# Gated feed-forward of a small transformer layer: the last 42 columns of gate and value as one block of weights

## The chip, the cores and the metric

The kernel runs on one core of one Trainium2 chip. The core has five engines that work side by side and wait for each other through semaphores: TensorE (PE in the profile; its weight loads are listed as PEld), VectorE (DVE), ScalarE (ACT), GpSimd (POOL) and SyncE (SP, which here only issues loads and stores). Matrix products land in PSUM, from where VectorE and ScalarE read them; everything else lies in SBUF. Each engine runs its instructions strictly in the order of the program. The metric is the device time of one execution in microseconds; the median of several runs is compared.

## The reference, cut to what matters

The whole computation is two layers of a model on 32 sequences of 64 positions and 256 channels, with a context of 1601 rows for each sequence. Layer 1 has a cross-attention over the context, then a block with a causal convolution, a gated recurrence and a gated feed-forward, then a quantised feed-forward. The change concerns the gated feed-forward alone:

```
FF_INNER = int(D * 4 * 2 / 3)          # D = 256, so 682
...
n = _rmsnorm(x, ff_gamma)
ff = jax.nn.silu(n @ w_gate) * (n @ w_value) @ w_ff_out
x = ff * RES_SCALE + x
```

`w_gate` and `w_value` are 256 x 682, `w_ff_out` is 682 x 256. The 682 inner channels are five blocks of 128 and a rest of 42.

## The kernel before, in words

The 2048 rows of x are cut into 16 tiles of 128 rows (two sequences each). They are processed in the order 1, 2, ..., 15, 0; this text calls them by these numbers. The long loop of the program runs over pieces of the context: 13 for each tile, each with a fixed order on TensorE: the scores with the maxima taken off (`s`, lines 770 and 776), the values of a later piece (`vps`), the scores by rows of a piece five ahead (`r`, line 728), whose maxima VectorE takes (line 735, `mx`), the weighted sums of values (`o`, line 800), and the keys of a piece six ahead (`kps`). `s` and `r` take turns in two buffers of PSUM of their own.

All other work of the two layers is written as generators that `yield` between their steps. A list named `plan` gives each generator a start, an end and a count of steps, and the loop runs the steps that are due at two places of each piece: between `vps` and `r`, and after `kps`. The order of instructions on TensorE, VectorE, ScalarE and GpSimd is the order in which this Python code runs; the scheduler moves nothing on these four. Only the order on SyncE is its own.

The work on several tiles is under way at once: while the gated block of tile t is computed, the first layer of tiles t+3 and t+4 and the query of tile t+3 are too, so that between `vps` and `r` there may stand, one behind the other, the feed-forward of one tile, the transposition `tp_d` (for the query) of another, and a step of a third.

The small products all take their PSUM tiles from one pool, `ps_mm`, of three buffers (`mm_tile`). A tile's buffer is given on when the last instruction that reads it has run. Which buffer the next tile is laid into, and so which reader its first matmul waits for, is settled when the program is built, by the building framework. In the program before, the second half's two tiles and the two that follow lie, for tile 1, in buffers 0, 1, 2 and 0: `ff_1_3_0` in 0, `ff_1_3_1` in 1, `tp_d` in 2, and `tp_c` again in 0, where it waits for the reading of line 235.

The gated feed-forward (generator `recurrent`, from line 938) works on `nT`, the normalised tile transposed: 128 channels x 2 chunks x 128 rows. The inner channels are padded from 682 to 6 x 128 (`NF` is 6); the padding of `w_fg` (gate) and `w_fv` (value) is zeroed once by GpSimd (line 1046), and the rest is loaded by SyncE (line 1056) in the function `late_weights`, in the first 40 us. The six blocks are done in two halves of three. For each half, one PSUM tile holds three blocks of gate sums and another three blocks of value sums (`ff_<tile>_<first block>_0` and `_1`). Each block is two matmuls (one for each chunk of channels, `mm2`), and each fp32 matmul is two records in the trace: 24 records a half. Then `silu_mul` (lines 234 to 238): ScalarE takes tanh of half the gate; VectorE halves the gate (line 235), multiplies it by the value (line 236), and after a `yield` by tanh + 1 (line 238). Since both read the same PSUM tile, VectorE's line 235 waits for ScalarE's line 234. At last `ffo` (line 951) multiplies the six blocks `m` by `w_fo`, whose rows beyond 682 are zero.

Of the kernel before, what the change touches and what calls it, by code (L numbers as in the profile page):

```python
# [9 lines left out]
F32 = mybir.dt.float32  # L10
BF16 = mybir.dt.bfloat16
AF = mybir.ActivationFunctionType
ALU = mybir.AluOpType
AX = mybir.AxisListType

P = 128
# [8 lines left out]
FF = 682  # L25
NF = 6
# [18 lines left out]
def perceiver_kernel(ctx: ExitStack, tc: tile.TileContext, a: dict, out: bass.AP):  # L45
    nc = tc.nc
    PSUM = bass.MemoryType.PSUM

    const = ctx.enter_context(tc.tile_pool(name="const", bufs=1))
# [20 lines left out]
    def mm_tile(shape, name, dtype=F32):  # L70
        return ps_mm.tile(shape, dtype, tag="mm", name=name)
# [111 lines left out]
    def moments(x, name):  # L183

        st = small.tile([P, 6], F32, tag="bnst", name=f"st_{name}")
        nc.vector.bn_stats(st, x)
        mv = small.tile([P, 2], F32, tag="bnmv", name=f"mv_{name}", bufs=4)
        nc.vector.bn_aggr(mv, st)
        rstd = small.tile([P, 1], F32, tag="rstd", name=f"rstd_{name}", bufs=4)
        nc.gpsimd.tensor_scalar(rstd, mv[:, 1:2], 1e-5, None, ALU.add)  # L190
        nc.gpsimd.tensor_tensor(rstd, rstd, mhalf, ALU.pow)
        return x, mv, rstd
# [34 lines left out]
    def mm2(o, lhsT, rhs):  # L227

        for c in range(2):
            nc.tensor.matmul(o, lhsT=lhsT(c), rhs=rhs(c), start=(c == 0), stop=(c == 1))  # L230

    def silu_mul(m, u, v, th):

        nc.scalar.activation(th, u, AF.Tanh, scale=0.5)
        nc.vector.tensor_scalar(m, u, 0.5, None, ALU.mult)
        nc.vector.tensor_tensor(m, m, v, ALU.mult)
        yield
        nc.vector.scalar_tensor_tensor(m, th, 1.0, m, ALU.add, ALU.mult)
# [611 lines left out]
    def recurrent(ti, x):  # L850
        def tile_(shape, tag, name):
            return work_tile(shape, tag, f"{name}_{ti}")

        m = moments(x, f"e{ti}")
# [8 lines left out]
        for c in range(2):  # L863
            nc.scalar.activation(ypad[:, c, :, 3:], t[:, c, :].rearrange("p (b s) -> p b s", b=2), AF.Copy,
                                 scale=gains[:, c, 0:1])
# [17 lines left out]
        nT = tile_([P, 2, P], "xTb", "nT")  # L883
# [14 lines left out]
        for part in range(2):  # L898
            for c in range(2):
                for h in range(2):  # L900
                    r = slice(64 * h, 64 * h + 64)
# [34 lines left out]
        nT = tile_([P, 2, P], "xTb", "nT2")  # L936
# [1 line left out]
            nc.scalar.activation(nT[:, c, :], t[:, c, :], AF.Copy, scale=gains[:, c, 2:3])  # L938
        yield ACT
        m = tile_([P, NF, P], "w4k", "fm")  # L940
        for f0 in range(0, NF, 3):
            uv = [mm_tile([P, 3, P], f"ff_{ti}_{f0}_{j}") for j in range(2)]
            for o, w in zip(uv, (w_fg, w_fv)):
                for f in range(3):
                    mm2(o[:, f, :], lambda c: w[:, c, (f0 + f) * P:(f0 + f + 1) * P], lambda c: nT[:, c, :])
            th = tile_([P, 3, P], "g2k", f"fth{f0}")
            yield from silu_mul(m[:, f0:f0 + 3, :], uv[0], uv[1], th)
            yield ACT if f0 == 0 else None
        o = mm_tile([P, D], f"ffo_{ti}")
        for f in range(NF):  # L950
# [54 lines left out]
    def tail(ti, x):  # L1005
        x = yield from recurrent(ti, x)
        yield from bit_ffn(ti, x)
# [32 lines left out]
    w_hg = const.tile([P, 2, 2 * DI], F32, name="w_hg")  # L1040
    w_go = const.tile([P, 4, 64], F32, name="w_go")
    nc.gpsimd.memset(w_go[DI:], 0.0)
    w_fg = const.tile([P, 2, NF * P], F32, name="w_fg")
    w_fv = const.tile([P, 2, NF * P], F32, name="w_fv")
    for w in (w_fg, w_fv):
        nc.gpsimd.memset(w[:, :, FF:], 0.0)
    w_fo = const.tile([P, NF, D], F32, name="w_fo")
    nc.gpsimd.memset(w_fo[:, NF - 1, :], 0.0)

    def late_weights():  # L1050
        nc.sync.dma_start(w_o2, a["L1_xattn_WoT"].rearrange("(c p) o -> p c o", p=P))
        nc.sync.dma_start(w_pw, a["L1_attn_pw_wT"].rearrange("(c p) o -> p c o", p=P))
        nc.sync.dma_start(w_hg, a["L1_attn_w_hg"].rearrange("(c h) d e -> (h d) c e", c=2))
        nc.sync.dma_start(w_go[:DI], a["L1_attn_w_out"].rearrange("h e o -> e h o"))
        for w, name in ((w_fg, "L1_attn_w_gate"), (w_fv, "L1_attn_w_value")):
            nc.sync.dma_start(w[:, :, :FF], a[name].rearrange("(c p) f -> p c f", p=P))
        last = (NF - 1) * P
        nc.sync.dma_start(w_fo[:, 0:NF - 1, :], a["L1_attn_w_ff_out"][0:last, :].rearrange("(f p) o -> p f o", p=P))
        nc.sync.dma_start(w_fo[0:FF - last, NF - 1, :], a["L1_attn_w_ff_out"][last:FF, :])

# [159 lines left out]
    with tc.manual_schedule(engines={ET.PE, ET.DVE, ET.Activation, ET.Pool}):  # L1220
# [43 lines left out]
        for g in range(NU * NT):  # L1264
            pos, p = divmod(g, NU)
# [79 lines left out]
```

## Time and profile before

| what | value |
|---|---|
| median of 3 runs | 2155.64 us (2155.49 to 2157.81) |
| the profiled execution's own time | 2154.58 us |
| its span, first to last instruction | 2152.9 us |
| TensorE busy / weight loads | 2034.8 us / 1482.9 us |
| VectorE, ScalarE, GpSimd busy | 1302.2, 907.1, 324.7 us |
| matmul records of ff (w_fg + w_fv) | 384 + 384 |
| L234 tanh, L235, L236, L238 on 128x384 | 490, 557, 553, 547 ns (median), 32 each |
| L236 on 128x256 (the first layer's `m`) | 421 ns |
| idle time of DVE before L235, ended by L234 | 44.4 us in 32 times |

A line of the timeline has the start and the duration in us, the engine, the line of the kernel, the operation, what it writes and what it reads, the shapes and the count of merged instructions; in brackets stands how long the engine had been idle before and who ended that. Matmuls overlap one another: the duration of one record is longer than its distance to the next. A row of a table by windows has the window, its length, the busy time of PE, PEld, DVE, ACT and POOL with their counts, the granted clock of TensorE (1.00 is full speed), the DMA engines' share and GB/s.

### The profile page before, as it was taken

The page shows a single profiled execution, that of the slowest core. Times are in us where ns is not written, and L with a number is a line of the kernel's source. Part 1 is how long each engine was busy: PE and PEld are TensorE (multiplying, and loading weights), DVE is VectorE, ACT ScalarE, POOL GpSimd, SP SyncE. Part 2 cuts the span into 40 slices and gives each one's busy share as a digit, 9 for nine tenths or more (in the row PEclk, how much of TensorE's full clock was granted, in tenths as well). Part 3 has the DMA queues.
Part 4 walks back from the last instruction along what each step waited for, and adds up shares of the span by engine and source line. Part 5 has one row for each costly group of instructions (what it writes and reads, how often), then busy time and mean ns, then how long its engine had stood idle before and what let it go on. Part 6 is the DMA issues. An engine that isn't in the chain of part 4 may idle for free.

```text
span 2152.9 us, 69473 instructions
## 1 busy us (share of the span) xinstructions
PE 2034.8 (95%) x31691; PEld 1482.9 (69%) x31707; DVE 1302.2 (60%) x2614; ACT 907.1 (42%) x1400; POOL 324.7 (15%) x538
## 2 busy tenths in 40 slices
PE   5799999999999999999999999999999999999964
PEld 4567677777776777777777777767776666676753
DVE  4556756666656665665666656565676656565544
ACT  3334454444535444444444435453433334334332
POOL 2211211111112111112111111111100111000011
PEclk8799999999999999999999999999999999999986
DMA  7233212221212222112221212211111111101000
GB/s 267 84 107 115 95 66 75 68 75 35 74 67 71 73 68 67 45 66 75 68 75 40 91 33 79 75 38 42 45 45 32 47 42 35 54 2 45 2 14 5
DMA packets 52654, 134.77 MB, mean 63 GB/s; under 512 B 12894, under 2 KB 32776, under 8 KB 52360
## 3 DMA queue, kind: packets, MB, share of 16 engines
q1 hardware_dynamic: 51800, 129.52, 17.6%
q8 instruction: 248, 4.06, 0.8%
q10 hardware_dynamic: 560, 0.81, 0.1%
q14 instruction: 46, 0.38, 0.1%
HBM read 124.02 MB, written 6.29 MB: 61 GB/s over the span
## 4 chain that ended last, share of the span: by engine, by line
PE 84%; DVE 9%; ACT 3%; DMA 2%; issue 1%; POOL 1%; SPq 0%; POOLq 0%; DVEq 0%; ACTq 0%
PE vps L230 17%; PE kps L230 16%; PE r L728 10%; PE o L800 9%; PE s L776 8%; PE ff L230 4%; DVE mx L735 3%; PE s L770 3%; PE ffo L951 2%; PE q L230 1%; ACT pt L782 1%; PE wo L230 1%; PE hg L902 1%; PE s L330 1%; PE v L316 1%
## 5 line engine op out<-in xcount | busy, mean ns | idle before, releaser
L735 DVE TENSOR_REDUCE mx<-r 128x2 f32<-128x1024 f32 x384 | 451.9, 1219 | 131.2 <-PE r L728 131.1
L782 ACT ACTIVATE pt<-s 128x1024 f32<-128x1024 f32 (+1 forms) x416 | 403.0, 1020 | 286.0 <-PE s L776 285.8
L695 ACT ACTIVATE kt<-kps,chv 128x512 f32<-128x512 f32 x192 | 131.9, 687 | 636.1 <-PE kps L230 636.1
L230 PE MATMUL kps<-ctxT,w_L_xattn_WkT 128*128 128x512 f32 x768 | 384.5, 624 | 11.9 <-DMA ctxT<-ctxT 11.9
L230 PE MATMUL vps<-w_L_xattn_WvT,ctxT 128*128 128x128 f32 x3072 | 394.5, 282 | 0.0
L230 PEld LDWEIGHTS vps<-w_L_xattn_WvT,ctxT 128*128 128x128 f32 x3072 | 358.5, 192 | 23.7 <-issue 2.8
L712 DVE COPY vau<-vps 128x512 f32<-128x512 f32 (+1 forms) x208 | 143.4, 689 | 370.4 <-PE vps L230 370.4
L800 PEld LDWEIGHTS o<-pt,vau 128*32 128x32 f32 (+1 forms) x13312 | 196.7, 110 | 151.5 <-issue 139.7
L800 PE MATMUL o<-pt,vau 128*32 128x64 f32 (+1 forms) x13312 | 231.2, 221 | 5.3 <-ACT pt L782 5.2
L728 PE MATMUL r<-kt,qbd 32*128 32x512 f32 x1536 | 230.3, 650 | 1.9 <-DVE mx L735 1.1
L230 PEld LDWEIGHTS kps<-ctxT,w_L_xattn_WkT 128*128 128x128 f32 x768 | 132.0, 191 | 124.4 <-issue 107.5
L776 PEld LDWEIGHTS s<-qbd,kt 32*128 32x128 f32 x6144 | 206.2, 187 | 3.1
L776 PE MATMUL s<-qbd,kt 32*128 32x128 f32 x6144 | 207.3, 271 | 0.0
L242 ACT ACTIVATE part<-part 128x1601 f32<-128x1601 f32 x60 | 92.6, 1543 | 16.9 <-DMA part<-ctxT 16.6
L728 PEld LDWEIGHTS r<-kt,qbd 32*128 32x128 f32 x1536 | 65.7, 185 | 40.8 <-issue 18.5
L770 PE MATMUL s<-neg,onesb 3*128 3x512 bf16 x768 | 80.4, 385 | 6.7 <-DVE mx L735 4.5
L770 PEld LDWEIGHTS <-onesb 3*128 3x128 bf16 x768 | 20.9, 91 | 94.2 <-issue 92.5
L230 PE MATMUL ff<-nT,w_fg 128*128 128x128 f32 x384 | 51.7, 287 | 1.0 <-ACT nT L938 1.0
L308 POOL TENSOR_TENSOR kbd<-kT,mask 128x512 f32<-128x512 f32 x32 | 32.7, 1043 | 129.9 <-ACT kT L301 129.9
L230 PEld LDWEIGHTS ff<-nT,w_fg 128*128 128x128 f32 x384 | 47.8, 200 | 1.9 <-ACT nT L938 1.8
L230 PE MATMUL ff<-nT,w_fv 128*128 128x128 f32 x384 | 48.9, 278 | 0.0
L230 PEld LDWEIGHTS ff<-nT,w_fv 128*128 128x128 f32 x384 | 46.5, 196 | 0.0
(329 smaller groups left out, 2435.7 us busy)
## 6 DMA issues: line engine op xcount, KB each, us to landing
ctxT<-ctxT SPq DMA_DIRECT2D x32, 1601.0 KB
part<-ctxT SPq DMA_DIRECT2D x60, 800.5 KB
od<-osb SPq DMA_DIRECT2D x16, 256.0 KB
rest<-ctxT SPq DMA_DIRECT2D x32, 65.0 KB
x<-x SPq DMA_DIRECT2D x16, 128.0 KB
rs<-od SPq DMA_DIRECT2D x32, 64.0 KB
og<-od SPq DMA_DIRECT2D x32, 64.0 KB
out<-x SPq DMA_DIRECT2D x16, 128.0 KB
```

The lines of the kernel that those rows point to most:

```text
L230: nc.tensor.matmul(o, lhsT=lhsT(c), rhs=rhs(c), start=(c == 0), stop=(c == 1))
L242: nc.scalar.activation(junk, src, AF.Copy, accum_out=csum[:, c, b:b + 1])
L308: nc.gpsimd.tensor_tensor(kbd[oc], kT[:, oc, :].rearrange("p (b k) -> p b k", b=2).unsqueeze(2).to_broadcast([P, 2, 4, S]), mask4.unsqueez ...
L695: nc.scalar.activation(kt, o, AF.Identity, bias=chv[:, hf.oc, BK2:BK2 + 1])
L712: nc.vector.tensor_copy(v[:kr, :, 0:VW - 16].rearrange("p k (h d) -> p k h d", d=17)[:, :, :, 0:16], o[:kr].rearrange("p k (h d) -> p k h ...
L728: nc.tensor.matmul(o, lhsT=qbd[r, q % 2, q // 2].rearrange("p h q -> p (h q)"), rhs=w.kt[r, q, :] if h is None else halves[h].kt[k][r, :], ...
L735: nc.vector.tensor_reduce(w.mx[:, 2 * m:2 * m + 2, h % 4, k], ps[m], AX.X, ALU.max)
L770: nc.tensor.matmul(o, lhsT=onesb[r, :], rhs=halves[h].neg[r, :].unsqueeze(1).to_broadcast([3, 4, P]), start=True, stop=False)
L776: nc.tensor.matmul(ps[i // 2][:kr, i % 2, j * P:(j + 1) * P], lhsT=w.kt[r, j, :] if h is None else halves[h].kt[k][r, j * P:(j + 1) * P], ...
L782: nc.scalar.activation(pt[:kr].rearrange("p i k c -> p i (k c)"), ps[m][:kr], AF.Exp)
L800: nc.tensor.matmul(w.o[32 * c:32 * c + 32, q, m, :], lhsT=v[:kr, j, 17 * hd:17 * hd + 32], rhs=pts[m][:kr, c // 2, j, c % 2 * S:c % 2 * S ...
L951: nc.tensor.matmul(o, lhsT=m[:, f, :], rhs=w_fo[:, f, :], start=(f == 0), stop=(f == NF - 1))
```

## The change

The first half (blocks 0 to 2) is computed as before, but written out in place of the call of `silu_mul`. The second half had three blocks of gate and three of value. Now it has two of each, and one block `w_fl` that holds both rests: the gate's last 42 columns in its columns 0 to 41 and the value's last 42 in its columns 64 to 105, zero elsewhere. Its product is the first of the half and goes into the third block of the gate's PSUM tile; so that block has gate sums in its partitions 0 to 41 and value sums in 64 to 105. Tanh and the halving still run over all three blocks. The product with the value is split: blocks 0 and 1 of the half as one instruction on 128 x 256, and the last block as a second one on 64 x 128, which multiplies partitions 0 to 63 of `m` by partitions 64 to 127 of the gate's PSUM tile. The upper partitions of that block of `m` meet rows of `w_fo` that are zero.

The weights shrink to five blocks each, with `w_fl` beside them. One memset of `w_fl` replaces two of padding. `late_weights` issues four loads where it had two; the two new ones have 42 columns, 168 bytes in a row.

```diff
-        for f0 in range(0, NF, 3):
+        for f0, n in ((0, 3), (3, 2)):
             uv = [mm_tile([P, 3, P], f"ff_{ti}_{f0}_{j}") for j in range(2)]
+            if f0:
+
+                mm2(uv[0][:, 2, :], lambda c: w_fl[:, c, :], lambda c: nT[:, c, :])
             for o, w in zip(uv, (w_fg, w_fv)):
-                for f in range(3):
+                for f in range(n):
                     mm2(o[:, f, :], lambda c: w[:, c, (f0 + f) * P:(f0 + f + 1) * P], lambda c: nT[:, c, :])
             th = tile_([P, 3, P], "g2k", f"fth{f0}")
-            yield from silu_mul(m[:, f0:f0 + 3, :], uv[0], uv[1], th)
+            u = uv[0][:, 0:3]
+            nc.scalar.activation(th, u, AF.Tanh, scale=0.5)
+            mf = m[:, f0:f0 + 3, :]
+            nc.vector.tensor_scalar(mf, u, 0.5, None, ALU.mult)
+            nc.vector.tensor_tensor(mf[:, 0:n], mf[:, 0:n], uv[1][:, 0:n], ALU.mult)
+            if f0:
+                nc.vector.tensor_tensor(mf[0:64, 2], mf[0:64, 2], uv[0][64:128, 2], ALU.mult)
+            yield
+            nc.vector.scalar_tensor_tensor(mf, th, 1.0, mf, ALU.add, ALU.mult)
             yield ACT if f0 == 0 else None
...
-    w_fg = const.tile([P, 2, NF * P], F32, name="w_fg")
-    w_fv = const.tile([P, 2, NF * P], F32, name="w_fv")
-    for w in (w_fg, w_fv):
-        nc.gpsimd.memset(w[:, :, FF:], 0.0)
+    w_fg = const.tile([P, 2, (NF - 1) * P], F32, name="w_fg")
+    w_fv = const.tile([P, 2, (NF - 1) * P], F32, name="w_fv")
+    w_fl = const.tile([P, 2, P], F32, name="w_fl")
+    nc.gpsimd.memset(w_fl, 0.0)
...
+        last = (NF - 1) * P
         for w, name in ((w_fg, "L1_attn_w_gate"), (w_fv, "L1_attn_w_value")):
-            nc.sync.dma_start(w[:, :, :FF], a[name].rearrange("(c p) f -> p c f", p=P))
-        last = (NF - 1) * P
+            ends = a[name].rearrange("(c p) f -> p c f", p=P)
+            nc.sync.dma_start(w, ends[:, :, :last])
+            r = 0 if w is w_fg else 64
+            nc.sync.dma_start(w_fl[:, :, r:r + FF - last], ends[:, :, last:])
```

In the changed kernel the lines of this part are 951 (tanh), 953 (halving), 954 (product with the value), 956 (the last block's product), 958 (product with tanh + 1) and 962 (`ffo`).

## The prediction

> **What bounds the kernel now.** I read the page first: the busy shares and the chain that ended last. TensorE is busy 95% of a 2152.9 us span and makes 84% of the chain, so an edit counts by what it does to TensorE's queue; VectorE (60%) and ScalarE (42%) count only where TensorE waits for them.
>
> ```profile
> PE 2034.8 (95%) x31691; PEld 1482.9 (69%) x31707; DVE 1302.2 (60%) x2614; ACT 907.1 (42%) x1400; POOL 324.7 (15%) x538
> ...
> PE 84%; DVE 9%; ACT 3%; DMA 2%; issue 1%; POOL 1%; SPq 0%; POOLq 0%; DVEq 0%; ACTq 0%
> ...
> L230 PE MATMUL ff<-nT,w_fg 128*128 128x128 f32 x384 | 51.7, 287 | 1.0 <-ACT nT L938 1.0
> ```
>
> The mean of 287 ns is no price: matmuls overlap. The timeline of a second half (tile 1) gives the pace, and what follows.
>
> ```profile
> 372.65 1.50 PE L230 MATMUL ff<-nT,w_fg 128*128 128x128 f32 x12
> ...
> 374.00 1.50 PE L230 MATMUL ff<-nT,w_fv 128*128 128x128 f32 x12
> 374.19 0.49 ACT L234 ACTIVATE fth<-ff 128x384 f32<-128x384 f32 x1 [1.32 <-PE ff L230]
> 374.72 0.56 DVE L235 TENSOR_SCALAR fm<-ff 128x384 f32<-128x384 f32 x1 [1.17 <-ACT fth L234]
> ...
> 375.33 0.38 PE L214 MATMUL tp_d<-ident,xn_d 128*128 128x128 f32 x2
> ...
> 375.54 0.56 DVE L236 TENSOR_TENSOR fm<-fm,ff 128x384 f32<-128x384 f32 x1 [0.26 <-PE ff L230]
> 375.55 0.38 PE L214 MATMUL tp_c<-ident,xn_c 128*128 128x128 f32 x2
> 375.75 0.37 ACT L220 COPY xT_d<-tp_d 128x256 f32<-128x256 f32 x1 [1.07 <-PE tp_d L214]
> ```
>
> 24 records fill 375.33 - 372.65 = 2.68 us, 0.1117 us each. The next PSUM tile, tp_d, is followed 0.22 us later by another, tp_c, with no wait: it lies in the buffer that gate sums ff_1_3_0 left when L235 ended (375.28).
>
> The third view is the timeline of a place where two PSUM tiles in a row share a buffer already: the second waits for ScalarE's copy of the first.
>
> ```profile
> 709.35 0.41 PE L214 MATMUL tp_c<-ident,xn_c 128*128 128x128 f32 x2
> ...
> 709.79 0.37 ACT L220 COPY xT_c<-tp_c 128x256 f32<-128x256 f32 x1 [0.38 <-PE tp_c L214]
> ...
> 710.22 0.44 PE L214 MATMUL tp_b<-ident,xn_b 128*128 128x128 f32 x2 [0.46 <-ACT xT_c L220]
> ```
>
> Start to start is 0.87 us instead of 0.22.
>
> **The change part by part.**
>
> *Matmuls.* The second half goes from 3+3 blocks to 1+2+2: 20 records for 24. Saved: 4 x 0.1117 = 0.447 us a tile, 64 records in all. The first PSUM tile still takes 12 records, so tanh (L234 of before) starts when it did; TensorE comes to tp_d at 2.235 us from the half's start instead of 2.68.
>
> *The buffer that comes free.* The gate's PSUM tile now has a third reader, L956, behind L954. The pool has three buffers, and by the buffers and waits that stand in the built programs it no longer gives this one to the tile after next: the tile behind tp_d is laid into tp_d's own buffer and waits for the copy xT_d on ScalarE. In before it waited for L235, long done. This is so in nine tiles: 1 and 8 (tp_c), 2 and 9 (su), 3 and 10 (v), 6 (tpp), 7 (o0), 12 (gps). In 4, 5, 11 and 13 only kps takes that buffer, two stages later (2.4 us after tp_d in before), when the copy has long ended; tile 14 has no tp_d. ScalarE is free for the copy: tanh ends 2.03 us after the half's start, and xT_d is next in its queue. So tp_d at 2.235, its successor at 2.235 + 0.87 = 3.105 us. Without the wait it stood at 2.90 in tiles 1, 2, 6, 8, 9 and at 2.99 in 3, 7, 10, 12 (0.09 more, since the array's shape changes there). After the idle time the two transposes of the row above took 0.37 us to the next issue (710.59) where an unhindered pair in the same place of tile 2's first half took 0.31: 0.06 more. Net: 5 x (3.105 + 0.06 - 2.90) = +1.3 us and 4 x (3.105 + 0.06 - 2.99) = +0.7 us. The five others gain 5 x 0.447 = 2.2 us. Bounds of the wait: none at all (all 14 tiles gain, 6.3 us), and 1.2 us of idle, the longest wait of TensorE for ScalarE in mid-run (L800), 0.74 more than here, 9 x 0.74 = 6.7 us more. I take 0.87, the row of the same two operations. Behind the waiting matmul stand r, o and kps; VectorE's maxima (L735) wait for r and s waits for them, so all move with TensorE and none absorbs the shift.
>
> *VectorE.* L236 on 384 columns takes 0.553 us; L954 on 256 takes 0.42, the row of m at L236. L956 (64x128) is not in the trace: between 0.16 (128x4, L744) and 0.42 (128x256); the straight line between them gives 0.29, and I take 0.3. So +0.17 us a tile. It hides behind L735, which waited 0.95 us for r in tile 1 and at least 0.73 in the other tiles I read (4 and 13); with that cover gone it would cost 16 x 0.17 = 2.7 us. L954 also starts sooner: 0.10 us after L235 (the gap of m's pair at 501.90 to 502.00) instead of 0.26.
>
> *The end.* In tiles 15 and 0 VectorE's chain L235, L236, L238 is on the path. Before, L236 of tile 0 ran to 2130.36; now 2129.61 + 0.10 + 0.42 + 0.02 + 0.30 = 2130.45: +0.1 us. Tile 15: 2094.22 to 2094.25. The saved records give nothing here: ffo waits for L238 anyway.
>
> *Loads, SP and memsets.* Two more issues on SP of 0.47 us (row of w_gate): SP is idle from 32.52 to 36.35 and from 39.87 to 44.49. Loads wait for the one eight places before, so the second rest load now waits for w_fg, issued at 30.63; SP has until 44.49. The bytes stay, but 512 packets of 168 B are added, 16 per DMA engine and load. The first load stands ahead of a context piece on whose landing ScalarE waits:
>
> ```profile
> 32.05 0.47 SPq L1056 DMA_DIRECT2D w_fv<-L_attn_w_value  x1
> ...
> 36.35 0.34 SPq L96 DMA_DIRECT2D part<-ctxT  x1
> ...
> 42.84 1.54 ACT L242 ACTIVATE part<-part 128x1601 f32<-128x1601 f32 x1 [0.62 <-DMA part<-ctxT]
> ```
>
> A packet's price: 0.06 us on ScalarE's queue (0.1% of 16 x 2152.9 us over 560), 0.117 on q1 (17.6% over 51,800); 16 packets are 1.0 to 1.9 us. Behind that sum ScalarE copies pT (44.56 to 45.14), which TensorE takes at 46.08: slack 0.9 us. Path cost 0 (if the packets overlap others) to 1.0; I take 0.1, the first queue's price, since its packets are smaller than q1's mean. The Trainium skill, page "DMA: Bandwidth & Descriptors", section Specifications, says that below 512 B a DMA engine does a read-modify-write; by it I estimate each packet at twice the price above, and the sum would be some 1 to 3 us longer. No row here prices such a packet. One memset for two (0.246 us each at 6 us) is covered until the load at 30.63.
>
> **Sum.** -2.2 + 1.3 + 0.7 + 0.1 + 0.1 = 0.0 us, against the profiled execution's own 2154.58 us (span 2152.9). That run lies 1.06 us under the median; so the median stays 2155.6.
>
> **The rivals.**
>
> *The wait does not bite* (the buffer is free in time, the change merely does what it says): 14 x 0.447 = 6.3 us less, 2149.4. For it: 64 records do go, on the bounding engine. Against it: the row at 709.35, where just such a wait idled TensorE 0.46 us.
>
> *The waits close the clock gate* (the other side): nine new idle gaps, and TensorE runs slow behind each. In tile 15 24 ff records after a wait took 4.62 us instead of 2.68: 1.94 us a closing, 9 x 1.94 = 17.5 us, 2173. It decides from three closings (5.8 us). For it: the granted clock was 0.54 in 80 to 100 us, with TensorE busy for 15.69 of 20. Against it: 1.00 in 620 to 740 us, which holds the wait at 710.
>
> ```profile
> 80.00:100.00 20.00, 15.69 (x85) 8.54 (x89) 12.24 (x16) 4.80 (x6) 2.42 (x2) 0.54 0.20 71
> 620.00:740.00 120.00, 117.96 (x1896) 86.37 (x1896) 79.92 (x171) 55.48 (x87) 19.45 (x31) 1.00 0.20 70
> ```
>
> The Trainium skill, page "TensorE: Matmul & The Clock Gate", section "A second HAM failure mode: psum-queue depth-cycling", tells of short idle gaps between groups of matmuls that were enough to make the gate oscillate; by that rule this rival would hold, and the window at 710 does not bear it out.
>
> *The small packets delay the start*: each of the two loads holds its part load up by 4.0 us, the longest wait of SP for od's write. Less the slack of 0.9, 3 us each: up to +6, 2161.8. Against it: the bytes are equal, and the DMA engines' share falls from 0.92 in 35 to 40 us to 0.65 and 0.47 in the next two 5 us.
>
> *VectorE's cover is gone*: +2.7 us, 2158.3; against it, the idle time ahead of L735.
>
> **How the numbers follow.** A measurement of this kernel tells about 0.2% (4.3 us) from no change. Forecast: 0.76, within. No wait: 0.10, faster. Clock gate: 0.05, slower. Small packets: 0.07, of which 0.05 slower. VectorE: 0.02, within. So faster 0.10, same 0.76 + 0.02 + 0.02 = 0.80, slower 0.10. Range: low end a wait of half its price (9 x 0.36 = 3.2 us less), 2152.4; high end the skew of the runs shown (+2.2), the packets' 1.0 and half of VectorE's 2.7, 2160. It leaves out the first two rivals and the slow part of the third, 2 in 10.
>
> **What would show it.** After: ff records 704 for 768; nine new TensorE waits on ACT's xT_d of some 0.4 us idle each (tp_c, su, v, tpp, o, gps), 3.7 us in all; successor of tp_d at 3.1 us in those tiles, r at 2.54 in 4, 5, 11, 13; sixteen L956 of 0.3 us; the first ff of tile 1 within 1 us of 360.8. The prediction is wrong if those waits are missing, if the clock falls behind them, or if the start is later by more than 2 us.

## The result and the profile after

The changed kernel takes 2153.23 us (median of 22 runs, 2152.16 to 2155.74) against 2156.34 us for the kernel before (22 runs beside it, 2153.72 to 2158.66): a ratio of 0.9986, 95% interval 0.9980 to 0.9993, or 3.0 us less (1.5 to 4.3). That is within the 0.2% that the prediction called no change, and within its range of 2152.4 to 2160.0. The predicted difference, however, was 0.0 us, and the interval leaves zero out. (Differences between versions go by the ratio from here on; the two medians can differ by up to 0.7 us more or less.) So there are two questions: did the records that went give their time back to a wait, as predicted, and where do the 3 us come from?

The profiled execution took 2154.06 us with a span of 2152.4 us. Its page's line of busy times:

```profile
PE 2031.1 (94%) x31627; PEld 1478.0 (69%) x31643; DVE 1305.3 (61%) x2630; ACT 907.2 (42%) x1400; POOL 324.6 (15%) x537
```

and the groups of ff in its table by line and shape:

```profile
L230 PE MATMUL ff<-nT,w_fg 128*128 128x128 f32 x320 | 44.6, 289 | 1.0 <-ACT nT L938 1.0
L230 PE MATMUL ff<-nT,w_fv 128*128 128x128 f32 x320 | 42.2, 280 | 0.0
...
L230 PE MATMUL ff<-nT,w_fl 128*128 128x128 f32 x64 | 9.8, 275 | 0.0
```

320 + 320 + 64 = 704 records of ff instead of 768. TensorE is busy 3.7 us less, VectorE 3.1 us more. The timeline of the second half of tile 1 is the place that the prediction is about:

```profile
372.36 0.61 PE L230 MATMUL ff<-nT,w_fl 128*128 128x128 f32 x4
...
373.90 0.49 ACT L951 ACTIVATE fth<-ff 128x384 f32<-128x384 f32 x1 [1.32 <-PE ff L230]
...
374.59 0.38 PE L214 MATMUL tp_d<-ident,xn_d 128*128 128x128 f32 x2
375.01 0.37 ACT L220 COPY xT_d<-tp_d 128x256 f32<-128x256 f32 x1 [0.62 <-PE tp_d L214]
375.08 0.42 DVE L954 TENSOR_TENSOR fm<-fm,ff 128x256 f32<-128x256 f32 x1
...
375.44 0.44 PE L214 MATMUL tp_c<-ident,xn_c 128*128 128x128 f32 x2 [0.46 <-ACT xT_d L220]
375.54 0.29 DVE L956 TENSOR_TENSOR fm<-fm,ff 64x128 f32<-64x128 f32 x1
375.80 0.31 PEld L728 LDWEIGHTS r<-kt,qbd 32*128 32x128 f32 x8 [0.17 <-issue]
```

tp_d comes 374.59 - 372.36 = 2.23 us after the half's start instead of 2.68: the four records are gone. Its successor tp_c stands at 3.08 instead of 2.90, behind a new idle time of 0.46 us that ScalarE's copy xT_d ended. The list of TensorE's waits from 110 to 2075 us has all nine (us in total, times, the longest); none of these lines is in the list of before:

```profile
PE tp_c L214 <- ACT xT_d L220: 0.9, 2, 0.5
PE su L230 <- ACT xT_d L220: 0.9, 2, 0.5
PE v L316 <- ACT xT_d L220: 0.9, 2, 0.5
...
PE tpp L370 <- ACT xT_d L220: 0.6, 1, 0.6
...
PE o L382 <- ACT xT_d L220: 0.5, 1, 0.5
PE gps L586 <- ACT xT_d L220: 0.5, 1, 0.5
```

Together 4.3 us (3.7 were predicted). From one tile's half to the next, the timelines give this for the start of r, the first work behind the small products, in us after the start of the half:

| tile | successor of tp_d, before and after | r, before and after | change |
|---|---|---|---|
| 1, 8 | 2.90, 3.08 | 3.21, 3.44 and 3.45 | +0.23, +0.24 |
| 2, 9 | 2.90, 3.08 | 6.57, 6.85 | +0.28, +0.28 |
| 3, 10 | 2.99, 3.08 | 4.02, 4.10 | +0.08, +0.08 |
| 6 | 2.90, 3.17 | 3.43, 3.73 | +0.30 |
| 7 | 2.99, 3.08 | 3.89, 3.81 | -0.08 |
| 12 | 2.99, 3.08 | 4.05, 4.13 | +0.08 |
| 4, 5, 11, 13 | none | 2.99, 2.54 or 2.55 | -0.44 or -0.45 each |
| 14 | none | 2.77, 2.33 | -0.44 |

The nine tiles lose 1.5 us, the five gain 2.2: the tiles come out at -0.7 us. That leaves more than 2 us of the middle value of 3.0 to find.

One more difference between the two traces is large and has no part of the change near it. Just before tile 14, in tile 13's piece, TensorE of the kernel before stops within a run of 32 equal matmuls. The timeline there:

```profile
1945.66 0.86 PE L776 MATMUL s<-qbd,ktr 32*65 32x128 f32 x24
...
1947.77 0.45 PE L776 MATMUL s<-qbd,ktr 32*65 32x128 f32 x8 [1.25 <-issue]
```

In the changed kernel the same 32 run through:

```profile
1945.07 1.07 PE L776 MATMUL s<-qbd,ktr 32*65 32x128 f32 x32
```

"Issue" is time in which the engine waited for nothing that the profile shows. The list of TensorE's waits of before, from 110 to 2075 us, has this stop as its only one of that kind; the list of the changed kernel has none:

```profile
PE s L776 <- issue: 1.3, 1, 1.3
```

From the first of the 32 to the next `vps`, 2.49 us became 1.01: the changed kernel gains 1.48 us here. The two profiled executions differ by only 0.5 us in the end because the changed one lost 1.8 us at 2067 to 2071 us, when its granted clock fell to 0.5 at 2064.3 us, before's at 2071.4.

### The profile page after: what moved, and what is told of

It is laid out like the page before. It is cut to its first block, busy times and chain, and to the rows that moved or that the text cites. A ratio compares the mean times of both kernels' runs of the same rounds, so it can differ in the third digit from the quotient of the medians.

```text
span 2152.4 us, 69363 instructions
## 1 busy us (share of the span) xinstructions
PE 2031.1 (94%) x31627; PEld 1478.0 (69%) x31643; DVE 1305.3 (61%) x2630; ACT 907.2 (42%) x1400; POOL 324.6 (15%) x537
## 3 DMA queue, kind: packets, MB, share of 16 engines
q8 instruction: 248, 4.06, 0.8%
## 4 chain that ended last, share of the span: by engine, by line
PE 84%; DVE 9%; ACT 3%; DMA 2%; issue 1%; POOL 1%; SPq 0%; POOLq 0%; DVEq 0%; ACTq 0%
PE vps L230 17%; PE kps L230 16%; PE r L728 10%; PE o L800 9%; PE s L776 8%; PE ff L230 4%; PE s L770 3%; DVE mx L735 3%; PE ffo L962 2%; PE q L230 1%; ACT pt L782 1%; PE wo L230 1%; PE hg L902 1%; PE su L230 1%; PE s L330 1%
## 5 line engine op out<-in xcount | busy, mean ns | idle before, releaser
L735 DVE TENSOR_REDUCE mx<-r 128x2 f32<-128x1024 f32 x384 | 452.1, 1220 | 129.5 <-PE r L728 129.4
L962 PE MATMUL ffo<-w_fo,fm 128*128 128x256 f32 x192 | 44.6, 380 | 2.2 <-DVE fm L958 2.2
L962 PEld LDWEIGHTS ffo<-w_fo,fm 128*128 128x128 f32 x192 | 36.1, 190 | 13.7 <-issue 6.7
L230 PE MATMUL ff<-nT,w_fg 128*128 128x128 f32 x320 | 44.6, 289 | 1.0 <-ACT nT L938 1.0
L953 DVE TENSOR_SCALAR fm<-ff 128x384 f32<-128x384 f32 x32 | 17.8, 558 | 44.4 <-ACT fth L951 44.4
```

Source lines behind the costliest of these rows:

```text
L735: nc.vector.tensor_reduce(w.mx[:, 2 * m:2 * m + 2, h % 4, k], ps[m], AX.X, ALU.max)
L962: nc.tensor.matmul(o, lhsT=m[:, f, :], rhs=w_fo[:, f, :], start=(f == 0), stop=(f == NF - 1))
```

## The experiments

The theory to be tested was: the third reader of the gate's PSUM tile moves the next tile into tp_d's buffer, and that wait eats what the records give in nine of fourteen tiles. Rivals: the wait is cheaper than priced; the gain comes from the loads at the start; the difference comes from events that change from run to run.

**The rests in the value's PSUM tile.** The same saving of records, but the gate's tile keeps two readers:

```diff
-            if f0:
-                mm2(uv[0][:, 2, :], lambda c: w_fl[:, c, :], lambda c: nT[:, c, :])
             for o, w in zip(uv, (w_fg, w_fv)):
+                if f0 and w is w_fv:
+                    mm2(o[:, 2, :], lambda c: w_fl[:, c, :], lambda c: nT[:, c, :])
...
-            nc.scalar.activation(th, u, AF.Tanh, scale=0.5)
-            nc.vector.tensor_scalar(mf, u, 0.5, None, ALU.mult)
+            nc.scalar.activation(th[:, 0:n], uv[0][:, 0:n], AF.Tanh, scale=0.5)
+            nc.vector.tensor_scalar(mf[:, 0:n], uv[0][:, 0:n], 0.5, None, ALU.mult)
+            if f0:
+                nc.scalar.activation(th[:, 2], uv[1][:, 2], AF.Tanh, scale=0.5)
+                nc.vector.tensor_scalar(mf[:, 2], uv[1][:, 2], 0.5, None, ALU.mult)
...
-                nc.vector.tensor_tensor(mf[0:64, 2], mf[0:64, 2], uv[0][64:128, 2], ALU.mult)
+                nc.vector.tensor_tensor(mf[0:64, 2], mf[0:64, 2], uv[1][64:128, 2], ALU.mult)
```

> The block of the two rests is laid into the value's PSUM tile instead of the gate's; it is multiplied between gate and value, and tanh and halving of it become instructions of their own (ScalarE one more, VectorE one more a tile). The gate's tile then has two readers, and the tile behind tp_d lies in its buffer again, as in before. Theory (the buffer eats what the records give): the successor of tp_d stands at about 2.45 us after the half's start in all tiles, no wait on xT_d is left, and all 14 tiles gain 0.447 us: 6.3 us under before, 5.8 under the changed kernel's sum by the traces (2154.06). Rival 1 (the wait costs only half of what I took; that is why the changed kernel came out 3.1 us faster): about 3 us under the changed kernel. Rival 2 (the gain of 3.1 us lies at the start, in the loads, and the wait eats all of the records): 9.4 us under before.

Measured: 2148.69 us against 2156.73 for before, ratio 0.9966 (0.9953 to 0.9978): 7.3 us less (4.7 to 10.1). It beats both kernels. Its timeline in tile 1:

```profile
373.88 1.06 PE L230 MATMUL ff<-nT,w_fg 128*128 128x128 f32 x8
...
375.39 0.42 DVE L951 TENSOR_SCALAR fm<-ff 128x256 f32<-128x256 f32 x1 [0.62 <-ACT fth L950]
...
376.12 0.38 PE L214 MATMUL tp_d<-ident,xn_d 128*128 128x128 f32 x2
...
376.34 0.38 PE L214 MATMUL tp_c<-ident,xn_c 128*128 128x128 f32 x2
...
376.65 0.71 PE L728 MATMUL r<-kt,qbd 32*128 32x512 f32 x4
```

tp_c stands 376.34 - 373.88 = 2.46 us after the start, 0.22 behind tp_d, and waits for nobody: its buffer came free when the halving of two blocks ended, at 375.81. r stands at 2.77 instead of 3.21. In all 14 tiles what follows is 0.45 us sooner, 6.25 us together, and no wait on xT_d is in the list. A second set of runs says the same:

> The version with the rests in the value's PSUM tile once more. Theory: 14 x 0.447 = 6.3 us from the records and 1.3 to 1.5 us from the missing stall at 1946 us: 7.6 to 7.8 us under before, no wait of TensorE on xT_d in the second halves.

Measured: 2147.32 us against 2155.09, ratio 0.9966 (0.9954 to 0.9979), again 7.3 us less (4.5 to 9.9). So the four records are worth what was worked out, where nothing takes their place. The sum of the traces is 6.25 from the tiles and 1.48 from the stop that is gone here too, less 0.5 at the end, which my expectation left out: tanh and halving of the last block are instructions of their own now, and in tiles 15 and 0, where TensorE waits for `m`, what follows comes 0.23 and 0.26 us later than in before. Rival 1 asked for a version 3 us under the changed kernel; by the two ratios to before (0.9966, and 0.9985 for the changed kernel in the same set of runs) it is 4.1 us under. The middle values alone don't tell 3 from 5.8; the table of the tiles does.

**The third reader alone.** The kernel before, all 24 records, with one more reading:

```diff
             nc.vector.tensor_tensor(mf, mf, uv[1], ALU.mult)
+            if f0:
+                junk = small.tile([64, P], F32, tag="junk3", name=f"junk3_{ti}", bufs=1)
+                nc.vector.tensor_scalar(junk, uv[0][64:128, 2], 0.5, None, ALU.mult)
```

> The kernel before, with one more reading of the gate's PSUM tile in the second half (VectorE, 64x128, behind the product with the value, into a tile that nothing reads; the computation is whole). 24 records stay. This moves the tile behind tp_d into tp_d's buffer in the same nine tiles as the change does, with nothing saved. Theory: tp_d at 2.68 us, its successor at 2.68 + 0.85 = 3.53 instead of 2.90 or 2.99: 5 x 0.63 + 4 x 0.54 = 5.3 us, with 0.3 us of VectorE at the end: 5.3 to 6.3 us slower than before. Rival 1 (half the price): about 3 us slower. If the wait costs nothing: within 0.5 us of before.

Measured: 2163.12 us, ratio 1.0031 (1.0020 to 1.0042): 6.7 us slower (4.3 to 9.1). The timeline:

```profile
374.86 0.38 PE L214 MATMUL tp_d<-ident,xn_d 128*128 128x128 f32 x2
...
375.64 0.29 DVE L954 TENSOR_SCALAR junk<-ff 64x128 f32<-64x128 f32 x1
...
375.70 0.44 PE L214 MATMUL tp_c<-ident,xn_c 128*128 128x128 f32 x2 [0.46 <-ACT xT_d L220]
```

tp_c starts 375.70 - 374.86 = 0.84 us behind tp_d instead of 0.22. The nine shifts of r add up to 5.5 us; tiles 15 and 0, where VectorE is on the path, add 0.5 us. So a reading of 0.29 us, whose result nobody uses, costs 5.5 us through the choice of a buffer in nine tiles where it is off TensorE's path. The wait is not cheaper than priced: rival 1, 3 us, lies below the interval and far below the sum of the shifts.

**The last reader sooner.** The changed kernel with its two products swapped, one run:

```diff
-            nc.vector.tensor_tensor(mf[:, 0:n], mf[:, 0:n], uv[1][:, 0:n], ALU.mult)
             if f0:
                 nc.vector.tensor_tensor(mf[0:64, 2], mf[0:64, 2], uv[0][64:128, 2], ALU.mult)
+            nc.vector.tensor_tensor(mf[:, 0:n], mf[:, 0:n], uv[1][:, 0:n], ALU.mult)
```

> The changed kernel with the last block's product (64x128) ahead of the product of the other two blocks, so that VectorE reads the gate's PSUM tile for the last time 0.42 us sooner. By the built program the tile behind tp_d then lies in the gate's buffer again in the nine tiles, and waits for that product. Theory: tanh ends at 2.03 us after the half's start, the halving at 2.62, the last block's product at 2.94; the successor of tp_d at 2.95 to 3.05 us instead of 3.08: a wait on VectorE in place of the wait on xT_d, 0.3 to 1.2 us gained in all. Rival (some other thing than the buffer's last reader holds the successor): it stays at 3.08.

Measured: 2153.85 us, one run, beside 2153.98 for one run of before. The wait changed its owner, as expected, but not its length:

```profile
375.11 0.29 DVE L955 TENSOR_TENSOR fm<-fm,ff 64x128 f32<-64x128 f32 x1
...
375.55 0.41 PE L214 MATMUL tp_c<-ident,xn_c 128*128 128x128 f32 x2 [0.48 <-DVE fm L955]
```

The product ended at 375.40 and tp_c started at 375.55, 3.10 us after the half's start: the 0.15 us between the two was not in my expectation, and the gain of 0.3 us or more did not come (over the 14 tiles 0.1 us). All nine waits have these 0.15 us; most waits of TensorE for VectorE in this trace end 0.05 us after VectorE does, and why these take 0.1 us more was not tested. For tp_c to run on unhindered, the gate's tile would have to be free at 2.45.

**The loads alone.** The kernel before with four loads in place of two:

```diff
-            nc.sync.dma_start(w[:, :, :FF], a[name].rearrange("(c p) f -> p c f", p=P))
+            ends = a[name].rearrange("(c p) f -> p c f", p=P)
+            nc.sync.dma_start(w[:, :, :last], ends[:, :, :last])
+            nc.sync.dma_start(w[:, :, last:FF], ends[:, :, last:])
```

> The kernel before, with only the loads of gate and value split into 640 and 42 columns (four for two). Theory: no more than 0.3 us either way (the trace of the changed kernel stands 0.33 us ahead of that of before from the start on, which may as well be chance). Rival 2 (the start gives the gain): 2 to 3 us faster. The small packets of the first forecast's rival: up to 6 us slower.

Measured: 2156.43 us, ratio 1.0002 (0.9993 to 1.0010). The interval allows 1.5 us less to 2.2 us more. So the 512 small packets show no cost and no gain; rival 2 (2 to 3 us faster) falls, and so does the prediction's third rival (up to 6 us slower).

**The changed kernel and the kernel before once more.** No edit.

> The changed kernel once more. Theory: tile for tile the same as its first profile (successor of tp_d at 3.08 us, nine waits), 0.6 us under before by the end of tile 13; what the median shows beyond that comes from events that vary from run to run (a TensorE stall at 1946 us in the profile of before, the moment near 2064 to 2071 us at which the granted clock falls), so that its median lies 0.5 to 3 us under that of before and a second profile differs from the first in these places alone. Rival 2: again 3 us or more under before, and the second profile ahead of before by that much already in the first 100 us.

Measured: 2153.98 us, ratio 0.9985 (0.9977 to 0.9994), 3.2 us less (1.3 to 5.0) where at most 3 were expected. Successors at 3.08 and 3.17 again, nine waits again. Its start was later than before's by 0.3 us at 72 us, where the first profile's was earlier by 0.3: the start is chance.

> The kernel before once more, to see which events return. Theory: the stall of 1.25 to 1.5 us at 1946 us is there again; short drops of the granted clock (3.4 us at half speed) are in other places than in its first profile; median within 1.5 us of before.

Measured: 2155.40 us, ratio 1.0001 (0.9992 to 1.0010). The stall is back, in the same run of matmuls and behind the same record:

```profile
1948.71 0.45 PE L776 MATMUL s<-qbd,ktr 32*65 32x128 f32 x8 [1.38 <-issue]
```

So it is no chance event. All four profiles with 24 records and an unchanged start of TensorE's program have it (before 1.25 us, before again 1.38, the third reader 1.51, the split loads 1.2), always with 24 of the 32 done; none of the five profiles with 20 records (after, after again, swapped, value tile twice) has it. In two of those five (after again, value tile again) the granted clock was at 0.5 for 3.4 us just there, at 1942.5 and 1939.8 us, and a run further down shows that a half clock at this place can hide the stop; the other three stood at full clock.

A queue that brings instructions has a row of its own in the profile. The page's list of queues (packets, MB, share of 16 engines), the same in both kernels:

```profile
q8 instruction: 248, 4.06, 0.8%
```

4.06 MB / 248 is 16,384 bytes a packet, and TensorE's 63,600 or so records over 248 packets are 256 each. In the packets' own records of before, one starts at 1933.66 us. After 256 more records of TensorE, at 1941.65, the next was due; it starts only at 1945.44, 437 records behind the one before. It lands at 1946.38, the last of the 24 matmuls ends at 1946.52, and TensorE goes on at 1947.77. From 1940.81 to 1946.4 us the packets of a context load, issued by SyncE at 1939.79, are under way. The table of windows has the DMA engines' share in the last column but one:

```profile
1939.79 0.37 SPq L101 DMA_DIRECT2D ctxT<-ctxT  x1
...
1941.00:1946.00 5.00, 4.57 (x125) 3.17 (x129) 2.92 (x5) 1.25 (x4) 1.61 (x3) 1.00 0.86 318
1946.00:1949.00 3.00, 1.75 (x35) 1.40 (x28) 0.00 (x0) 0.91 (x2) 0.77 (x2) 1.00 0.03 8
```

In the changed kernel the block of 256 ends elsewhere: 13 tiles with 8 records fewer (four matmuls, four weight loads) make 104. There the packet, due at 1942.41 under the same load, starts at 1944.81, 313 records behind the one before, and is in time. The Trainium skill, page "Runtime: NRT & Kernel Launch", section "Instruction fetch mechanics", says that an engine's instructions are refilled in blocks of 256 by a DMA queue of its own, and that crossing a block is mostly hidden: the packets here agree with the size, and in before 247 of the 248 left no stop of more than 0.2 us. If this is the cause, moving the block's end must make the stall go and come. Both were tried, with matmuls whose sums nobody reads, ahead of TensorE's first real one:

```diff
+        if not shifted:
+            shifted.append(g)
+            for _ in range(38):
+                nc.tensor.matmul(o[:, 0:64], lhsT=ident, rhs=ident[:, 0:64], start=True, stop=True)
         mm2(o, lambda c: w_k2[:, c, hf.oc * P:(hf.oc + 1) * P], ...
```

> The kernel before with 38 more fp32 matmuls (152 records) ahead of its first real one, in the first 11 us; the computation is whole. 152 = 256 - 104: the instruction stream at tile 13 stands against the packets of 256 as in the changed kernel. Theory: the packet at 1945 us is late by less than 130 records, there is no stall at 1946 us, 1.3 to 1.5 us faster than before. Rival: the stall stays, the time of before.

Measured: 2160.14 us, ratio 1.0021 (1.0012 to 1.0029). As a time it was no gain but 4.5 us more: the added matmul records took 0.22 us each and put the first real product at 17.8 us, 5.9 us later, which I had not foreseen. But the stall is gone. The same place:

```profile
1950.31 1.07 PE L782 MATMUL s<-qbd,ktr 32*65 32x128 f32 x32
...
1951.32 0.41 PEld L230 LDWEIGHTS vps<-w_L_xattn_WvT,ctxT 128*128 128x128 f32 x3 [0.17 <-issue]
```

The packet came 355 records behind the one before it. This kernel lies 4.65 us behind before at the first of the 32 (1950.31 against 1945.66) and 3.17 behind it at the next `vps` (1951.32 against 1948.15): 1.48 us regained, the same amount as in the changed kernel, with all that follows the added matmuls as in before.

> A second look at the kernel before with 152 more records ahead. Theory: no stall at 1946 us, as in its first look. Rival: its absence was chance, the stall is there.

Measured: 2155.23 us, one run; no stall in s at 1946 us again (packet 337 records behind the one before, 1.5 us regained).

> The changed kernel with 26 more fp32 matmuls (52 matmul and 52 weight-load records) on TensorE ahead of its first real one, in the first 11 us, in which it waits for a load; their sums are overwritten by the first real ones, the computation is whole. They put the instruction stream at tile 13 back where it stood before the change (13 tiles x 8 records fewer = 104). Theory (the rest of the gain is an instruction refill: TensorE's instructions come in packets of 256, one comes late at 1945 us behind a context load, and with 24 records TensorE runs dry there for 1.25 to 1.5 us, with 20 not): the packet at 1945 us is late by about 170 records, the stall of 1.2 to 1.5 us in s (line 776) at 1946 us is back, and the tiles stand as in the changed kernel: 1.3 to 1.5 us slower than it. Rival (the stall hangs on something else, such as the waits or the order in tile 13): no such stall, the time of the changed kernel.

Measured: 2154.92 us, ratio 0.9997 (0.9988 to 1.0006), 2.4 us over the changed kernel by the two ratios. This one did not do what it was made for: the packet came late as in before (458 records behind the one before it), but the granted clock was at 0.5 from 1942.9 to 1946.3 us, TensorE used its instructions at half the pace, and no stall is there. A stall came in another place instead, where this shift has put another block's end:

```profile
PE vps L230 <- issue: 1.1, 1, 1.1
```

That is at 680.2 us. So of the 2.4 us, some 1.1 are the start (the first real product at 12.66 instead of 11.61 us) and 1.1 are this stall.

> A second look at the changed kernel with 104 more records ahead. In the first look the granted clock was at 0.5 from 1942.9 to 1946.3 us, just where the stall was expected, so that TensorE used up its instructions at half pace. Theory: with the full clock there, the packet near 1946 us is late by about 170 records and the stall of 1.2 to 1.5 us in s (line 776) is there. Rival: no stall there.

Measured: 2155.02 us, one run. The clock fell at 1942.5 us again, the packet came 442 records behind the one before, there was no stall in s, and the one in vps was there again. That the stall comes back at 1946 us in the changed kernel is therefore not shown; that it goes in the kernel before is, twice, and that a shift makes one elsewhere is, twice.

Two more figures of these traces tie all six stalls, the four in s and the two in vps, to the packets. TensorE goes on 1.26 to 1.40 us after the late packet has landed, each time. And the place is that of a block's end: counted from the start of the program, 58,804 to 58,818 records stand ahead of the first one behind the stall in s, 19,391 and 19,394 ahead of that in vps, and each of these numbers is 180 to 194 more than a multiple of 256 (up to some 16 records are missing from a trace). By the same count the miss is explained: in the two runs of the changed kernel with 104 more records, TensorE at half clock came to the end of that block only 1.2 to 1.7 us after the packet had landed, and went on without a stop. What holds the packet up is read from the times alone: a context load is under way in all six cases (DMA share 0.78 and 0.74 from 674 to 679 us ahead of the two stalls in vps), but no run moved the load.

## Why the prediction was right or wrong

**The saved records (right).** 704 for 768, tp_d at 2.23 us for a predicted 2.235; five tiles gain 2.2 us as predicted.

**The wait (right, a little too dear).** The nine places, the releaser and the idle time of 0.46 us are as predicted; the successor stands at 3.08 for a predicted 3.105. The nine tiles lose 1.5 us, not 2.0. Half of the difference is tile 7: the step took r to move as its first successor o0 does, but in before tp_a behind o0 already waited 0.26 us (idle time of the weight load) for the same copy xT_d. In the changed kernel o0 waits and tp_a does not, so the tile gains 0.08. Most of the rest is tiles 3, 10 and 12: they lose 0.08 each and not 0.18. The sum added 0.06 there for two transposes behind the wait, but what waits in these three is another kind of product.

**VectorE and the end (right).** L956 took 290 ns (0.3), L954 on 256 columns 422 ns (0.42). In tile 0, from the last tanh to the last product with tanh + 1, 1.86 us became 1.94: +0.08 for +0.1. The cover held: L735's idle time is 129.5 us in all, 131.2 in before.

**The loads (no cost seen).** The 0.1 us was too small for the measurement: 1.0002 with the loads alone, and the first ff of tile 1 at 360.46 us (before 360.76). The 1 to 3 us more that the prediction estimated by the Trainium skill's rule on packets under 512 B did not show; the interval leaves room for up to 2.2.

**The clock (right).** The granted clock stayed at 1.00 over the waits; the window that was read against the rival now holds one of the nine waits (v, at 628 us), and the table still has 1.00:

```profile
620.00:740.00 120.00, 117.50 (x1889) 85.73 (x1889) 80.06 (x171) 55.15 (x87) 19.46 (x31) 1.00 0.20 70
```

The rule of the Trainium skill on short idle gaps, which the prediction cites, is not borne out here: no profile with the nine waits has a drop of the clock at any of them.

**What failed: the sum lacked a term.** It costed every instruction that goes by what stands beside it, and took the rest of TensorE's program as unmoved. But 104 records fewer by tile 13 also move the ends of the blocks of 256 in which TensorE's instructions arrive, and the packet for one such end came late under a context load, at a price of 1.25 us of idle time, 1.48 us from before to after. The line stood in before's list of TensorE's waits, and I had not read it. With it the sum is -2.2 + 1.5 + 0.1 - 1.5 = -2.1 us, within both intervals (1.5 to 4.3 and 1.3 to 5.0 us less). What the middle values have beyond that, about 1 us, is not settled. That the time still fell into the range is in part luck: the low end was set 3.2 us down for a cheaper wait, which did not come, and the missing term used that room.

**The reference.** I put the median at 2155.6 from the three runs shown; later sets of 22, 24 and 27 runs of the same kernel gave 2156.34, 2156.73 and 2155.09. The forecast of no change was right by the bound of 0.2%, and its middle value lay 2.4 us over the changed kernel's median. That 0.0 us were forecast and 3.0 measured does not come from this: both compare versions run side by side.

## What to carry to other kernels

Before adding a reader to a PSUM tile of a rotating pool, look at which buffer the next tiles get in the built program: one reading of 0.29 us cost this kernel 5.5 us in nine waits, and putting the new block into the tile that is read last anyway gave back all that the saved matmuls are worth. Read the line "issue" in the busiest engine's list of waits: here such a stall hung on where the blocks of its instructions end, so an edit ahead of it that changes the number of instructions can take it away or bring one, and a gain or loss of 1.1 to 1.5 us from it says nothing on the edit itself.

## What was not expected of the hardware

TensorE can run dry of instructions, for 1.06 to 1.51 us in these traces, when the packet that brings the next 256 comes late; each time a data load was under way. The matmuls that were added cost more than expected as well: 52 fp32 matmul records of 128x64 took 11.35 us at the start of the program, 0.22 us each.

The granted clock also drops for 3.4 us at a time, to 0.5, and where it does so differs between executions of one kernel. Between 120 and 2060 us, before has a drop at 1678.9 us in one profile and at 154.2, 1185.0 and 1949.6 in the other; the version with the value's tile has none in one and drops at 154.6, 427.7, 1178.6, 1677.0 and 1939.8 in the other. In the 3.5 us ahead of each of these nine drops TensorE was busy for 2.1 to 2.6 us only; but an equally idle stretch can keep the clock, such as 1946 to 1949 us in before (1.75 of 3.00 us, clock 1.00). A drop makes what follows some 1.6 us later (after again against before, at 1187 us). A pair of profiles can't be compared to better than a few of these unless the drops are counted first.
